# The second pair of batches boards one expert later, and an odd batch's last steps run without the next batch's first ones

## The chip, the cores and the metric

The kernel runs on one core of a Trainium2 chip. The metric is device time in microseconds of one execution, given as the median of several runs; less is better. One execution was also taken by the hardware profiler, and every row of a profile shown here comes from such an execution. TensorE is called PE in the rows (PEld for its weight loads), VectorE DVE, ScalarE ACT, GpSimd POOL, and SyncE, which issues nearly all DMAs, SP.

## What is computed

The input is x, 16 batches of 256 tokens by 256 channels, in float32. Four layers are added to it, one after the other:

```
x = x + L0(x)   # gates, 16 exponential moving averages over the tokens ("traces"), projections, layernorm
x = x + L1(x)   # masked softmax pooling over the 256 tokens of the batch
x = x + L2(x)   # 8 experts and a shared one, each silu(x Wg) * (x Wu) times Wd, width 1024, mixed by gates
x = x + L3(x)   # gelu(x W1 + b1) times W2, the last 64 columns with a matrix chosen by the batch
```

L0 and L1 need the tokens of one batch in order. L2 and L3 are matrix products with the same weights for all batches.

## The kernel before

Every float32 operand of a matrix product is split into a rounded part and a remainder, and each product is made of three matmuls (`mm3`, lines 101 to 103). The helper `rnd` (L88 on ACT) makes the rounded part, `low` (L95 on DVE or POOL) the remainder. Since all splits go through these helpers, rows are told apart by their tiles.

**The front end: steps.** For each batch b, L0 and L1 are two generators that yield after each step. `traces(b)` has 21 steps: the split of x and a scan (1), matmuls ph (2) and pm with a small store mdd (3), the gate matmuls pg with their activation and product gp (4), then sixteen steps with products bt (L359), scans tr (L363) and a running sum ta on POOL (L367), and a last split t (21). `pooled(b)` has 10 steps: matmuls pt (1), split s (2), matmuls po and statistics (3), x1 (L441, 4), transposes ptr (5), pa (6), psc and the exponentials (7), the normalisation (8), transposes ppt and the split q (9), and matmuls pp (L505 to L507), the sum acc (L509) and the split of acc, called x in the rows, its remainder on POOL (10). Except for batch 0, all PSUM results of these steps except the gate's gp share one tile with one buffer (tag `ps`).

**The back end: the plan.** L2 and L3 are a list of 640 items. An L2 item multiplies two 128-wide chunks of an expert's width by one batch, or one chunk by a pair of batches (512 columns either way). Its gate activation is L607, its product with the second half L608; its second matrix product comes two items later (`LAG`). An L3 item (activation L610) is an eighth of the last layer for a pair. Weight chunks arrive in a ring of ten buffers (`RING`), in the plan's order. On the first two uses of an expert's chunk it is loaded raw (raw_e, two buffers) and split; at the second it is stored split (keep_e), and from then on loaded split.

Experts go round in positions 0, 1, 2 ..., with position mod 9 the expert. A batch or a pair of batches boards at some position and rides nine positions, so that riders at the same position share the chunks. Batch 0 rides alone in positions 0 to 4, batches 0 and 1 together in 5 to 8, batch 1 alone in 9 to 13. Pair k (batches 2k and 2k+1) boards here:

```python
p0 = SECOND + NX * ((k - 1) // 2) + (0 if k % 2 else APART)
```

with NX = 9, APART = 5 and SECOND = 9. After a pair's last expert come its eight L3 items. Items are counted from 0 here, in the order of the plan; pair 1 boards at item 56, pair 2 at 128, pair 3 at 200, pair 5 at 360, pair 7 at 520.

**The order of the work.** The list `phases` says which steps are mixed: an entry with two generators takes steps of both in proportion (`feed`). `pace` gives how many steps follow each item, so that the steps due by `ready[b]` are done `SLACK` = 16 units of weight (an L2 item weighs 4, an L3 item 3) before the odd batch b boards. Where the next item is one of the first `HOLD` = 3 of an L3 group, no steps are given out. Each step's instructions are tied to come after the last item's product (`issue_after`); within that, a scheduler that works with its own estimate of times orders each engine's queue.

Of the kernel before, what the change touches and what calls it, by code (L numbers as in the profile page):

```python
# [23 lines left out]
FRONT = 4  # L24
SLACK = 16
L0_BUFS = {"bt": 3, "tr": 3, "mod": 2, "hA": 2, "hB": 2}
SECOND = 9
APART = 5
STORE = 2
LAG = 2  # L30
# [14 lines left out]
def fused_kernel(  # L45
# [662 lines left out]
    for k in range(1, NB // 2):  # L708
        p0 = SECOND + NX * ((k - 1) // 2) + (0 if k % 2 else APART)
        rides.append((p0, p0 + NX, (2 * k, 2 * k + 1)))  # L710
# [41 lines left out]
    phases, alone, ready = [[(traces, 0)]], {}, []  # L752
    count = FIRST
    for b in range(NB):
        more = b + 1 < NB
        phases.append([(pooled, b)] + [(traces, b + 1)] * more)
        count += STEPS["pooled"]
        if more and (b == 0 or b % 2):
            alone[len(phases) - 1] = FRONT
            phases.append([(traces, b + 1)])  # L760
            ready.append(count + FRONT)
            count += STEPS["traces"]
        else:
            count += STEPS["traces"] * more
            ready.append(count)
# [207 lines left out]
```

## Time and profile before

| | |
|---|---|
| median of 3 runs | 2857.16 us (2855.82 to 2858.89) |
| the profiled execution's own time | 2854.52 us |
| its span, first to last instruction | 2852.3 us |
| mean granted TensorE clock in it | 0.993 |
| PE busy / PEld busy | 2781.6 us (98%) / 2339.8 us (82%) |
| DVE / ACT / POOL busy | 1442.2 / 1239.2 / 1295.4 us |
| w_e loads from keep_e, of 768 KB each | 216 |
| raw_e loads, of 384 KB each | 144 |

Busy times are sums over the span, in which stages with different limits follow each other. A row of a timeline gives the start in us, the length in us, the engine, the line, the operation, the tiles written and read, and in brackets the idle time before it and what ended it. A row of waits gives who waited on whom, the total in us, how many times, and the longest.

### The profile page before, as it was taken

The page shows a single profiled execution, that of the slowest core. Times are in us where ns is not written, and L with a number is a line of the kernel's source. Part 1 is how long each engine was busy: PE and PEld are TensorE (multiplying, and loading weights), DVE is VectorE, ACT ScalarE, POOL GpSimd, SP SyncE. Part 2 cuts the span into 40 slices and gives each one's busy share as a digit, 9 for nine tenths or more (in the row PEclk, how much of TensorE's full clock was granted, in tenths as well). Part 3 has the DMA queues.
Part 4 walks back from the last instruction along what each step waited for, and adds up shares of the span by engine and source line. Part 5 has one row for each costly group of instructions (what it writes and reads, how often), then busy time and mean ns, then how long its engine had stood idle before and what let it go on. Part 6 is the DMA issues. An engine that isn't in the chain of part 4 may idle for free. (4 is left out here: it accounts for less than half of the span.)

```text
span 2852.3 us, 36958 instructions
## 1 busy us (share of the span) xinstructions
PE 2781.6 (98%) x13632; PEld 2339.8 (82%) x13632; DVE 1442.2 (51%) x2661; ACT 1239.2 (43%) x2054; POOL 1295.4 (45%) x984
## 2 busy tenths in 40 slices
PE   6889889999999999999999999999999999999999
PEld 4887778888888888888888888888888888888887
DVE  7978866665665454444544445444444542222222
ACT  5565544456444533435334443344433453233433
POOL 4755544544645453543534445344454443333333
PEclk8999999999999999999999999999999999999999
DMA  3444546547443532323433143332523242222552
GB/s 106 132 144 137 162 149 217 176 144 244 149 159 120 172 123 100 118 80 92 173 105 125 40 167 117 107 118 66 181 100 110 93 159 98 89 89 76 189 196 86
DMA packets 114694, 371.24 MB, mean 130 GB/s; under 512 B 12642, under 2 KB 30930, under 8 KB 114514
## 3 DMA queue, kind: packets, MB, share of 16 engines
q1 hardware_dynamic: 113650, 368.74, 39.0%
q8 instruction: 108, 1.77, 0.3%
q14 instruction: 72, 0.59, 0.1%
q10 hardware_dynamic: 864, 0.14, 0.0%
HBM read 304.62 MB, written 64.21 MB: 129 GB/s over the span
## 5 line engine op out<-in xcount | busy, mean ns | idle before, releaser
L95 POOL TENSOR_TENSOR hh<-h,hh 128x512 fp32r<-128x512 f32 x640 | 848.4, 1326 | 1327.1 <-ACT hh L88 1307.4
L608 DVE TENSOR_TENSOR h<-h,pu 128x512 f32<-128x512 f32 x576 | 393.9, 684 | 939.6 <-PE pu L103 818.1
L88 ACT ACTIVATE hh<-h 128x512 fp32r<-128x512 f32 x640 | 403.5, 631 | 932.6 <-DVE h L608 912.4
L101 PE MATMUL pg<-x,w_e 128*128 128x512 f32 (+1 forms) x1232 | 467.3, 379 | 12.7 <-ACT x L88 5.4
L607 ACT ACTIVATE h<-pg 128x512 f32<-128x512 f32 x576 | 342.9, 595 | 306.6 <-PE pg L103 228.5
L101 PE MATMUL pu<-x,w_e 128*128 128x512 f32 (+1 forms) x1232 | 465.4, 378 | 6.5 <-ACT h L607 3.7
L103 PE MATMUL pg<-x,w_e 128*128 128x512 f32 (+1 forms) x1232 | 465.7, 378 | 4.2 <-DVE w_e L95 3.4
L102 PE MATMUL y<-hh,w_e 128*128 128x512 f32 (+1 forms) x1232 | 464.4, 377 | 3.2 <-POOL hh L95 3.2
L102 PE MATMUL pg<-x,w_e 128*128 128x512 f32 (+1 forms) x1232 | 465.3, 378 | 0.0
L103 PE MATMUL pu<-x,w_e 128*128 128x512 f32 (+1 forms) x1232 | 463.8, 376 | 0.0
L102 PE MATMUL pu<-x,w_e 128*128 128x512 f32 (+1 forms) x1232 | 463.6, 376 | 0.0
L103 PE MATMUL y<-hh,w_e 128*128 128x512 f32 (+1 forms) x1232 | 463.5, 377 | 0.0
L101 PE MATMUL y<-hh,w_e 128*128 128x512 f32 (+1 forms) x1232 | 415.6, 377 | 1.0 <-DVE acc L655 0.8
L367 POOL TENSOR_TENSOR ta<-ta,tr 128x512 f32<-128x512 f32 x225 | 308.4, 1371 | 67.6 <-DVE tr L363 53.9
L363 DVE TENSOR_TENSOR_SCAN tr<-decay,bt 128x256 f32<-128x256 f32 x450 | 285.1, 672 | 0.0
L101 PEld LDWEIGHTS pg<-x,w_e 128*128 128x128 f32 x1232 | 232.5, 189 | 56.4 <-ACT w_e L88 6.4
L101 PEld LDWEIGHTS pu<-x,w_e 128*128 128x128 f32 x1232 | 232.1, 188 | 50.5 <-ACT h L607 5.8
L103 PEld LDWEIGHTS pg<-x,w_e 128*128 128x128 f32 x1232 | 232.7, 189 | 47.8 <-DVE w_e L95 5.2
L102 PEld LDWEIGHTS y<-hh,w_e 128*128 128x128 f32 x1232 | 233.0, 189 | 47.0 <-POOL hh L95 5.5
L101 PEld LDWEIGHTS y<-hh,w_e 128*128 128x128 f32 x1232 | 231.5, 189 | 44.8 <-ACT hh L88 1.3
L103 PEld LDWEIGHTS y<-hh,w_e 128*128 128x128 f32 x1232 | 233.0, 189 | 41.7
L103 PEld LDWEIGHTS pu<-x,w_e 128*128 128x128 f32 x1232 | 232.3, 189 | 41.9
(294 smaller groups left out, 3267.5 us busy)
## 6 DMA issues: line engine op xcount, KB each, us to landing
w_e<-keep_e SPq DMA_DIRECT2D x216, 768.0 KB, 4.4
raw_e<-in_wexp_dram SPq DMA_DIRECT2D x144, 384.0 KB, 4.5
keep_e<-w_e SPq DMA_DIRECT2D x72, 768.0 KB, 4.2
mod<-mdd SPq DMA_DIRECT2D x120, 256.0 KB, 3.5
w_f<-keep_f SPq DMA_DIRECT2D x56, 384.0 KB, 3.6
raw_c<-in_comb_dram SPq DMA_DIRECT2D x32, 260.0 KB, 2.8
xr<-in_xT_dram SPq DMA_DIRECT2D x16, 256.0 KB, 3.1
xt<-in_x_dram SPq DMA_DIRECT2D x16, 256.0 KB, 2.7
```

Source lines behind the costliest of these rows:

```text
L88: last_of["ca"] = A.activation(out_, in_, AF.Copy)
L95: i = (V if e == "v" else G).tensor_tensor(out_, in_, h.bitcast(F32), ALU.subtract)
L101: PE.matmul(o, wh, xh, start=start, stop=False, **kw)
L102: PE.matmul(o, wh, xl, start=False, stop=False, **kw)
L103: last_of["pe"] = PE.matmul(o, wl, xh, start=False, stop=stop, **kw)
L363: V.tensor_tensor_scan(tr[:, c], decay[:, d : d + 1].to_broadcast([P, S]), bt[:, c], 0.0, ALU.mult, ALU.add)
L367: G.tensor_tensor(tacc, tacc, tr, ALU.add)
L607: A.activation(h, ps_g, AF.Silu)
L608: last_of["h"] = V.tensor_tensor(h, h, ps_u, ALU.mult)
```

## The change

Two things are edited. `SECOND` goes from 9 to 10, so that pairs 1, 3, 5 and 7 as well as 2, 4 and 6 have a position that is one higher, and the plan has 46 positions in place of 45. And the entry of `phases` for `pooled(b)` with odd b no longer holds `traces(b + 1)`: those four steps (`FRONT`) come with the other 17 in the entry that follows. `ready` for odd b becomes four steps smaller. Batch 0 keeps its mixed entry, and so do the even batches.

```diff
-SECOND = 9
+SECOND = 10
...
     for b in range(NB):
         more = b + 1 < NB
-        phases.append([(pooled, b)] + [(traces, b + 1)] * more)
+        phases.append([(pooled, b)] + [(traces, b + 1)] * (more and (b == 0 or b % 2 == 0)))
         count += STEPS["pooled"]
         if more and (b == 0 or b % 2):
-            alone[len(phases) - 1] = FRONT
+            if b == 0:
+                alone[len(phases) - 1] = FRONT
             phases.append([(traces, b + 1)])
-            ready.append(count + FRONT)
+            ready.append(count + FRONT * (b == 0))
             count += STEPS["traces"]
         else:
             count += STEPS["traces"] * more
```

## The prediction

> **What bounds the kernel now.** I read the page first, then engine windows, then the waits and the timeline where TensorE stands still.
>
> ```profile
> span 2852.3 us, 36958 instructions
> ...
> PE 2781.6 (98%) x13632; PEld 2339.8 (82%) x13632; DVE 1442.2 (51%) x2661; ACT 1239.2 (43%) x2054; POOL 1295.4 (45%) x984
> ...
> PE   6889889999999999999999999999999999999999
> ```
>
> TensorE bounds the span, except in the first six or seven of 40 slices. The windows give the stages, and a stretch near the end in which no steps run:
>
> ```profile
> 76.00:198.00 122.00, 106.77 (x799) 100.17 (x798) 100.92 (x171) 72.04 (x113) 82.44 (x54) 0.97 0.48 144
> 198.00:360.00 162.00, 150.02 (x697) 119.90 (x696) 140.70 (x230) 86.96 (x141) 93.92 (x66) 0.99 0.47 149
> 360.00:380.00 20.00, 20.00 (x159) 19.48 (x158) 13.03 (x24) 12.30 (x21) 9.29 (x8) 1.00 0.60 197
> 380.00:404.00 24.00, 15.05 (x73) 12.61 (x73) 12.89 (x32) 6.31 (x12) 4.62 (x4) 0.79 0.20 64
> 404.00:718.00 314.00, 312.76 (x1765) 274.05 (x1763) 201.88 (x349) 163.08 (x269) 154.66 (x113) 1.00 0.56 190
> ...
> 2407.00:2668.00 261.00, 261.00 (x1153) 216.20 (x1152) 60.21 (x101) 81.47 (x134) 82.84 (x65) 1.00 0.26 85
> ```
>
> The columns are length, busy PE, PEld, DVE, ACT, POOL, granted clock, DMA share, GB/s. The worst window is 380 to 404: PE 15 of 24, PEld half, clock 0.79, and no other engine busy either: a chain of waits. To place it I count gate activations (L607; L610 in the last layer): the nth in time belongs to plan item n. Items 528 to 591 (2406.8 to 2667.9) run without steps, 64 in 261 us: an expert item costs **4.08 us**. Items 464 to 479 take 68.9 us with 12 steps: a hidden step costs TensorE (68.9 - 65.3)/12 = **0.3 us**. Item 55 has its gate at 375.3, item 56, the first of batches 2 and 3, at 404.1: **28.8 us in place of 4.1**.
>
> ```profile
> POOL x L95 <- ACT x L88: 19.4, 1, 19.4
> DVE gp L308 <- ACT gp L306: 6.5, 1, 6.5
> ACT gp L306 <- PE pg L103: 6.0, 1, 6.0
> ...
> PE pg L101 <- ACT x L88: 3.4, 1, 3.4
> ...
> PE pg L101 <- DVE q L95: 1.9, 1, 1.9
> ...
> PE pp L505 <- ACT gp L306: 1.0, 1, 1.0
> ```
>
> These are waits in that window (us, times, longest). POOL, ACT and PE all wait for x, the split of batch 3's sum. Why it is late, the timeline tells:
>
> ```profile
> 387.43 0.55 PE L101 MATMUL pg<-x,wh 128*128 128x256 f32 x1 [1.90 <-DVE q L95]
> ...
> 393.77 0.39 PE L505 MATMUL pp<-q,v 128*128 128x256 f32 x1 [1.02 <-ACT gp L306]
> ...
> 394.48 2.44 DVE L359 SCALAR_TENSOR_TENSOR bt<-gp,bl,mod 128x256 f32<-128x256 f32 x6
> ...
> 397.44 0.73 DVE L509 TENSOR_TENSOR acc<-x1T,pp 128x256 f32<-128x256 f32 x2
> ...
> 398.90 1.28 POOL L95 TENSOR_TENSOR x<-acc,x 128x512 fp32r<-128x512 f32 x1 [19.43 <-ACT x L88]
> ```
>
> The probabilities q are split at 387.3, but ahead of batch 3's last product pp stand the 24 gate matmuls pg of batch **4** (387.4 to 392.7), their activation, which frees the single PSUM tile, and on DVE batch 4's bt and scan work. pp starts at 393.8, the sum ends at 398.2. That foreign step costs batch 3's last step some **7 us**.
>
> **What the skill says.** "Perfetto Trace Analysis", section Matmuls, asks that independent groups rotate through PSUM banks; here traces and pooled share one tile (tag ps), and "PE pp <- ACT gp" above is that. Its section Sequencer Loop has an engine's instruction wait in its queue for semaphores; agreed: pp stands behind pg. "TensorE: Matmul & The Clock Gate", section What's actually happening, says an idle window of about 3.4 us halves the clock; agreed: clock 0.79, and pg matmuls of 256 columns stand 0.21 us apart at 388 against 0.12 for pp at 394. So a TensorE pause costs more than its length.
>
> **Part 1, boarding one expert later.** I worked plan, due times and steps through by hand from the listing. There are 640 items in both, total weight 2496. Batch 1's four items with expert 1 move ahead of pair 1, which boards at item 60 in place of 56; its eight shared items turn up after batch 0 and 1's last layer, as items 112 to 119. Pair 2 and all later ones board at the same item as before (128, 200, 288 ...). Cost: one expert position more (46 for 45), so eight more w_e loads of 768 KB, from the kept copy. The page has w_e loads at 4.4 us to landing, the DMA share in 2407 to 2668 is 0.26: taken as 0, at most 8 x (4.4 - 4.08) = 3 us if that cover went. A second cost lies in items 52 to 59, eight alone in a row, each two chunks of the ring, all split afresh. In the first stage, with the same diet, items 4 to 15 take 79.2 us, 6.6 each, and ACT waits for raw loads:
>
> ```profile
> ACT w_e L88 <- DMA raw_e<-in_wexp_dram: 51.0, 40, 3.5
> ```
>
> (waits of 76 to 360). The ring's ten chunks cover the first four; the other four I price at 6.6: 4 x (6.6 - 4.6) = 8 us; lower bound 0, if the ring is full, upper 16.
>
> **Part 2, no trace steps beside odd batches.** For b = 3, 5 ... 13 and 1, four steps of traces(b+1) move behind pooled(b): 32 PE matmuls (6 ph, 2 pm, 24 pg), 7 ACT activations, 6 DVE and one POOL operation, on SP the small mdd store, and the x loads of batch b+2 are asked ten steps later. Nothing vanishes: the same 488 steps. The moved work costs 0 where PE is full, the cover being the expert items; its loads (2.7 to 3.1 us landing) have a whole traces stage of 21 steps before use. In pair 1's wait it is worth the 7 us above. The pace falls as well: steps due by item 16 are 54 for 58, and until pair 1 boards (116 - 54)/(224 - 64) per unit of weight for (120 - 58)/(208 - 64), 1.55 per item for 1.72. DVE is busy 87% from 198 to 360, so fewer steps relieve it: item 49 has 105 steps behind it for 115. At TensorE's 0.3 us the ten are worth 3 us. At DVE's share, 140.7 less 32 items x 1.9 us (product 0.68 and chunk split 1.19, by their rows), over 55 steps, 1.45 us each, they are worth 14; but five of them fall in the first stage, which the chunk loads hold: 7. I take 6.
>
> **The sum for pair 1.** Item 49 comes at 345.9 - 6 = 340. Pooled 3 now has its steps in items 49 to 55. It began 29 us behind its item before (item 44 at 324, first pt at 352.7), dragged by pooled 2 in the DVE-bound stage; I take 15 (5 to 29). Its chain took 45.5 us (352.7 to 398.2), less 7: 38. From the sum to the gate took 5.9. So gate 60 comes at 340 + 15 + 38 + 6 = **399** (389 to 413). The TensorE side: eleven items from 49 at 4.6 are 51, and 8 for chunks: 399 too. So the wait should nearly close. Before, gate 60 came at 417.9: 19 earlier. Take off the seven steps still owed (120 for 127 at item 60), 2 us; pair 2's wait, items 120 to 127 in 43.1 us for 35, of which 5.7 come back right after, is worth 2 more, since pooled 5 stands free of traces(6). **19 us.** The profiled execution, 2854.5 with its span of 2852.3, becomes 2835.5; the median lies 2.7 above it: **2838**.
>
> **Rivals.** *A, forecast, 55%:* as summed, 2826 to 2847. *A', 6%:* half of it stays, 2848 to 2851.
> *B, the wait moves, 12%:* pooled 3 starts four items later in the plan; with the full 29 us lag and no 7 us saved, gate 60 comes at 340 + 29 + 45 + 6 = 420; two are owed, and 3.5 come back as they do today (gates 56 to 60 lie 13.8 apart for 17.3): no change, 2857. For it: lags of 35 to 50 us in pooled 2. Against: fewer steps, and pg gone from ahead of pp. That a planner orders each engine anyway, so that the trace steps were not the cause, ends here too.
> *C, slower, 17%:* the odd batches from 7 on. Pooled 7 had three steps before the last layer's hold; now all ten come in items 186 to 195, pair 3 boarding at 200. It has 963 to 1016, 5.2 us a step. Pooled 15, alone today, runs steps 4 to 10 in 2329.9 to 2362.1, 5.4 us each, and boards without a wait; but pooled 7 took 9.5 beside traces(8). Each us a step beyond 5.2 costs pairs 3, 5 and 7 some 10 + 8 + 9 us: from 5.9 the gain is gone; at 6.5, 35 - 19 = 16 us slower, 2873.
> *D, more, 10%:* the early lag vanishes and the chunks are in time: gate 60 at 389, with DVE's full relief of 14 at 381: 37 less the two owed: 2822.
>
> **The numbers.** A measurement of this kernel can tell 0.2%, 5.7 us, from no change. Faster: A, A' and D, 0.71; same: B, 0.12; slower: C, 0.17. The range 2818 to 2860 leaves out most of C and a tail of D.
>
> **What would show it.** Right: 224 w_e loads from keep_e for 216; gate 60 near 399, and no gap over 12 us from 55 to 60; no pg matmul between ppt and pp of batch 3; clock over 0.9 from 380 to 404; gate 128 some 19 us before 718.4. Wrong: gate 60 past 410, or ACT's waits for raw_e in front of items 56 to 59; and for C, gate 200 further from gate 128 than today's 302.6 us, with acc last.

## Result: 0.5% slower, where 0.7% faster was forecast

The changed kernel takes 2870.43 us in the median of six runs, against 2855.64 us for the kernel before in runs beside it: a ratio of 1.0049 (95% interval 1.0038 to 1.0059), some 14 us slower. One of the six runs took 7168.18 us; the ratio leaves it out, and the other five lie between 2868.65 and 2871.61. The forecast was 2838, with 2818 to 2860 as its range. The profiled execution of the change took 2871.61 us; its times below come from that one. First the page, lines as shown of the kernel before:

```profile
span 2869.7 us, 36970 instructions
...
PE 2786.8 (97%) x13632; PEld 2341.3 (82%) x13632; DVE 1441.6 (50%) x2661; ACT 1250.3 (44%) x2060; POOL 1297.0 (45%) x984
...
PE   6898989999999999999999999999999999999999
```

The same 13632 matmuls and the same DVE work take 17.4 us more. ACT is busy 11 us longer, 7.7 us of it in six more loads of its function tables (106 for 100, of 1.28 us each). PE is busy 5.2 us longer with the same matmuls; the other 12 us of the span are time in which it stood still. As forecast, there are 224 w_e loads from keep_e. The windows (columns as before: length, busy PE, PEld, DVE, ACT, POOL, granted clock, DMA share, GB/s):

```profile
76.00:198.00 122.00, 107.00 (x799) 99.04 (x799) 95.68 (x152) 73.31 (x113) 80.63 (x53) 1.00 0.45 138
198.00:360.00 162.00, 150.22 (x696) 120.50 (x695) 142.30 (x236) 84.20 (x133) 94.70 (x67) 0.98 0.48 149
...
398.00:425.00 27.00, 18.21 (x91) 15.84 (x90) 9.79 (x22) 12.71 (x25) 7.06 (x5) 0.75 0.43 144
```

DVE does 5.2 us less up to 198 us than before (95.7 for 100.9) and no less after that. And the pause in which no engine is full, which was to close, is still there, from 398 to 425, with the clock at 0.75. From 380 to 404 the clock is 1.00, as the forecast's signs asked, but only because the pause has moved. Who waits from 398 to 425:

```profile
POOL x L95 <- ACT x L88: 13.7, 1, 13.7
ACT x L88 <- DVE acc L509: 4.3, 1, 4.3
```

It is the same wait as before, for the split of batch 3's sum, and pair 1 is again what it holds up. Rows of the changed kernel's timeline (start, length, engine, line):

```profile
375.84 0.74 DVE L509 TENSOR_TENSOR acc<-x1T,pp 128x256 f32<-128x256 f32 x2
...
377.98 0.28 PE L101 MATMUL pt<-t,wh 128*128 128x256 f32 x1
...
398.67 0.58 ACT L607 ACTIVATE h<-pg 128x512 f32<-128x512 f32 x1
...
414.99 0.58 PE L505 MATMUL pp<-q,v 128*128 128x256 f32 x1 [1.81 <-DVE q L95]
...
417.95 0.75 DVE L509 TENSOR_TENSOR acc<-x1T,pp 128x256 f32<-128x256 f32 x2 [3.02 <-PE pp L507]
...
418.76 0.58 PE L101 MATMUL ph<-x,wh 128*128 128x256 f32 x1 [0.84 <-DVE acc L509]
...
424.94 0.60 ACT L607 ACTIVATE h<-pg 128x512 f32<-128x512 f32 x1
```

Batch 2's sum ends at 376.6 (before, at 348.4), batch 3's pooling begins at 378.0 (352.7) and takes 40.7 us to its sum at 418.7 (45.5). So the second edit does locally what it says: batch 4's first matmul ph now stands behind batch 3's sum, no foreign matmul stands ahead of pp. But the whole front end arrives some 25 us late. Gate 59 is at 398.7, gate 60 at 424.9: 26.3 us between two items, as there were 28.8 at item 55 before.

Where does the delay begin? At batch 2's start. The change first, then the kernel before (ph is the first matmul of batch 2's head, gp the end of its four first steps):

```profile
188.46 0.38 PE L101 MATMUL ph<-x,wh 128*128 128x256 f32 x1
...
209.38 0.69 DVE L308 SCALAR_TENSOR_TENSOR gp<-gp,xr 128x512 f32<-128x512 f32 x1
```

```profile
146.18 0.28 PE L101 MATMUL ph<-x,wh 128*128 128x256 f32 x1
...
180.29 0.69 DVE L308 SCALAR_TENSOR_TENSOR gp<-gp,xr 128x512 f32<-128x512 f32 x1
```

Batch 2's gated input is ready 29 us later. The edit of `phases` holds for b = 1 too, and b = 1 lies in the stage where TensorE is not the bound.

Against before, gate 60 is 7.0 us later, gate 128 5.1 (19 earlier was forecast), gate 144 12.8, gate 288 17.8, and from 528 on 17.4. So less than half of the loss is there at pair 1. From 430 to 2700 us PE stands still for 9.3 us, before for 2.3, and most of that is in three waits ahead of the last layer's second product z; before, no such wait is over 0.6 us:

```profile
630.21 0.47 PE L101 MATMUL z<-hh,w_f 128*128 128x512 f32 x1 [3.35 <-DVE acc L655]
...
1353.48 0.47 PE L101 MATMUL z<-hh,w_f 128*128 128x512 f32 x1 [2.06 <-DVE acc L655]
...
2035.61 0.47 PE L101 MATMUL z<-hh,w_f 128*128 128x512 f32 x1 [1.74 <-DVE acc L655]
```

### The profile page after: what moved, and what is told of

It is laid out like the page before. It is cut to its first block, busy times and chain, and to the rows that moved or that the text cites. A ratio compares the mean times of both kernels' runs of the same rounds, so it can differ in the third digit from the quotient of the medians.

```text
span 2869.7 us, 36970 instructions
## 1 busy us (share of the span) xinstructions
PE 2786.8 (97%) x13632; PEld 2341.3 (82%) x13632; DVE 1441.6 (50%) x2661; ACT 1250.3 (44%) x2060; POOL 1297.0 (45%) x984
```

## The experiments

The theories' numbers in the expectations: 1, that batch 3 just follows the pace set for it; 2, that the phases cost; 3, that eight lone items in a row hold the front end. Theory 2 later splits into 2a (the head behind batch 1's pooling, by its order), 2b (the later odd batches) and 2c (the due count of steps before pair 0 boards, `ready` of batch 1). Times stand against the kernel before, run beside them; its medians lay between 2854.28 and 2854.93.

**One edit at a time.** e1 has SECOND = 10 alone, e2 the phases alone (with their `ready`).

> SECOND = 10 alone, phases as before. Theory 1 (the pace follows the boarding: steps are given out so that batch 3 is done just before its item, and run some 43 us late, so a boarding four items later makes batch 3 four items later): acc of batch 3 ends at 412 to 422, gate 60 at 418 to 430, time +5 to +15 us against before. Theory 2 (the loss comes from the phases, odd batches without mixed trace steps): gate 60 at 395 to 408, time -5 to -20 us. Theory 3 (eight items alone in a row, with their 16 fresh chunk splits, hold DVE and ACT): gate 60 at 415 to 425 as well, time +5 to +10; run e3 tells it from theory 1.

Measured: 2846.92 us, ratio 0.9974 (0.9965 to 0.9982), 7 us faster. Batch 3's sum ends at 410.4, gate 60 is at 415.4.

> The new phases and ready with SECOND = 9. Theory 1: batch 3 boards at item 56 as before, its last step no longer behind batch 4's gate matmuls: acc of batch 3 ends at 388 to 396, gate 56 at 394 to 402, time 0 to -8 us. Theory 2: acc of batch 3 not before 405, gate 56 at 411 or later, time +5 to +15. Theory 3: as theory 1.

Measured: 2868.40 us, 1.0046 (1.0029 to 1.0063), 14 us slower. Batch 3's sum at 405.7, gate 56 at 411.6. Boarding later is a gain with the old phases and none with the new ones; the phases are the loss, with either boarding. That is theory 2, though e1's batch 3 is later than it said.

**The pace for pair 1.** e3 and e4 move batch 3's due time back to 208, e3 with the old phases, e4 with the new.

```diff
-    due = [(at[boards[b]] - SLACK, ready[b]) for b in range(1, NB, 2)]
+    due = [(at[boards[b]] - SLACK - 16 * (b == 3), ready[b]) for b in range(1, NB, 2)]
```

> SECOND = 10, phases as before, and the due time of batch 3 moved 16 units earlier, to 208, so that all steps up to item 52 are given out after the same items as before. Theory 1: acc of batch 3 ends at 396 to 404, as before (398.2), gate 60 at 402 to 410, time -8 to -16 us against before. Theory 3: batch 3's chain is held by the chunk splits of items 52 to 59: acc at 408 or later, gate 60 at 414 or later, time 0 to +8. Theory 2 says as theory 1 here.

Measured: 2844.90 us, 0.9967 (0.9955 to 0.9980), within noise of e1. Batch 3's sum ends at 409.6, not at 396 to 404; that is where theory 3 put it, but the time is not what theory 3 said.

> The whole change, with batch 3's due time back at 208. Theory 1: acc of batch 3 at 390 to 402, gate 60 at 396 to 408, time -5 to -18 us against before, 20 to 30 below the change. Theory 2: little better than the change, +8 to +14 against before. Theory 3: 0 to +8.

Measured: 2867.46 us, 1.0040 (1.0027 to 1.0052). Batch 3's sum at 418.0, as in the change. Giving the steps of batches 2 and 3 out earlier brings batch 3's sum forward by under 1 us in both: theory 1 falls.

**Which odd batches.** Four kernels with SECOND = 10 take the trace steps away beside some batches only: e6 beside 1, e7 beside 3, e8 beside 5 to 13, e9 beside 3 to 13. The edit of e7, against the kernel before, SECOND left out:

```diff
+        mix = more and not (b == 3)
-        phases.append([(pooled, b)] + [(traces, b + 1)] * more)
+        phases.append([(pooled, b)] + [(traces, b + 1)] * mix)
...
-            alone[len(phases) - 1] = FRONT
+            if mix:
+                alone[len(phases) - 1] = FRONT
...
-            ready.append(count + FRONT)
+            ready.append(count + FRONT * mix)
```

> SECOND = 10, and the trace steps are taken away beside batch 1 alone; beside batches 3 to 13 they stay. Theory 2a (the first four trace steps are a serial head of some 30 us that ran beside batch 1's pooling; put behind it they delay the whole front end, which has no slack until pair 1 boards): first sixteen-step product of batch 2 at 214 to 220 for 188, pooled 2 ends at 374 to 378 for 357 in e1, gate 60 at 425 to 440, time +8 to +20 us against e1, so 0 to +13 against before. Theory 2b (the loss is beside the later odd batches): within 3 us of e1, -4 to -10 against before.

Measured: 2863.29 us, 1.0030 (1.0020 to 1.0039), 16 us over e1. gp of batch 2 at 208.7, batch 2's sum at 376.8, gate 60 at 432.8, as theory 2a said.

> SECOND = 10, and the trace steps are taken away beside batch 3 alone. Theory 2a: pooled 3 starts as in e1 (358) and its chain falls from 52 us to 27 to 41, acc of batch 3 ends at 385 to 400; gate 60 at 396 to 408, time -14 to -24 us against before. Theory 2b: a loss against e1, so 0 to -5 against before.

Measured: 2839.06 us, 0.9946 (0.9930 to 0.9963), 16 us faster than before and 8 below e1. Batch 3's sum ends at 391.1, and the wait at pair 1 is gone. Pooled 3's first matmul, batch 3's sum, and gates 59 and 60 (of an execution that took 2835.03 us, the fastest of the four):

```profile
342.07 0.28 PE L101 MATMUL pt<-t,wh 128*128 128x256 f32 x1
...
390.41 0.74 DVE L509 TENSOR_TENSOR acc<-x1T,pp 128x256 f32<-128x256 f32 x2
...
392.80 0.58 ACT L607 ACTIVATE h<-pg 128x512 f32<-128x512 f32 x1
...
398.18 0.60 ACT L607 ACTIVATE h<-pg 128x512 f32<-128x512 f32 x1
```

The time and the gate are as theory 2a said, the way there is not: pooled 3 starts at 342.1, not 358, and takes 49.0 us, not 27 to 41 (e1: 357.9 and 52.5).

> SECOND = 10, and the trace steps are taken away beside batches 5 to 13, where TensorE has expert items to fill every wait. Theory 2a: nearly nothing there, within 3 us of e1, -4 to -10 against before; the gates of the change drift away by 6 us or so between items 144 and 448 as compared with before, and if that comes from these batches, it is +4 to +8 against e1, 0 to +1 against before. Theory 2b: +15 or more against e1.

Measured: 2854.66 us, 1.0000 (0.9991 to 1.0009), 7 us over e1: not nothing, so the drift of the change's gates does come from these batches.

> SECOND = 10, and the trace steps are taken away beside batches 3 to 13, not beside batch 1: the change without its effect on batch 1. Theory 2a: the forecast's own case, gate 60 at 396 to 408, time -8 to -22 us against before. Theory 2b: slower than e1 by 10 or more, so 0 to +8 against before.

Measured: 2847.45 us, 0.9974 (0.9963 to 0.9984): e7's gain less what e8 lost, and 1 us short of theory 2a's range. Gate 60 is at 402.0, near the 399 that the forecast summed.

So the edit of the phases is three things, each measured alone against e1: +16 us beside batch 1, -8 beside batch 3, +7 beside the later ones. They don't simply add: their sum is 16 us, and the change is 23.5 us over e1. One part of the difference shows in gate 60. Beside batch 3 the edit brings it forward by 17.2 us from e1 to e7, but the change, where batch 2's head is late, has it only 7.9 us before e6.

**Batch 1: order or due count?** e10 and e11 are e7 with three and eight trace steps beside batch 1 in place of four. e12 takes the steps away beside 1 and 3, but keeps 58 steps due before pair 0 boards.

> e7 with three trace steps beside batch 1 in place of four: the gate step of batch 2 goes behind batch 1's pooling. Theory 2a (serial head): that step and the way from it to the first product take some 16 us, so the first of batch 2's products comes at 200 to 206 for 186 in e7, gate 60 6 to 12 us later than 398, time +5 to +12 us against e7 (2839), so -3 to -11 against before. Theory 2c (it is the lower pace of the first 16 items, 54 steps for 58, that costs): one step of four, +4 or less against e7.

Measured: 2843.36 us, 0.9957 (0.9940 to 0.9973), 4 us over e7, though the runs of the two overlap. gp of batch 2 at 183.7 for 178.2; gate 60 at 402.3. That is nearer theory 2c.

> e7 with eight trace steps beside batch 1 in place of four, 62 steps due by the same item. Theory 2a: the head ran fully beside the pooling already; four more steps bring batch 2's products 5 to 10 us forward but load DVE before pair 0 boards: within 6 us of e7 either way, -10 to -22 against before. Theory 2c: a higher early pace helps again, 5 us or more below e7.

Measured: 2839.02 us, 0.9945 (0.9928 to 0.9961): as e7. gp of batch 2 at 154, 24 us earlier, and yet batch 3's sum ends at 395.1. That is theory 2a's case: what is gained at batch 2's head is lost again by then.

> No trace steps beside batches 1 and 3, SECOND = 10, and the steps due by the first boarding set to 58 as in the kernel before, so that the early pace is the old one. Theory 2a: batch 2's head still starts only when batch 1's pooling ends; the quicker pace may bring that end up to 5 us forward; first product at 205 to 216, time +6 to +16 against e7, so -9 to +1 against before. Theory 2c: back at e7 within 3 us, -13 to -18 against before.

Measured: 2843.18 us, 0.9957 (0.9941 to 0.9974), 4 us over e7. Batch 1's pooling, alone, begins at 126.9 and its sum ends at 168.2; gp of batch 2 at 184.2. Neither theory had this: the order costs 4 us (e7's runs lie between 2835.03 and 2840.29, e12's between 2840.65 and 2844.19), and the due count should cost more than that. Two kernels separate them.

```diff
# e14: the change, and
-            ready.append(count + FRONT * (b == 0))
+            ready.append(count + FRONT * (b == 0) + 4 * (b == 1))
# e15: SECOND = 10, the old phases, and
-            ready.append(count + FRONT)
+            ready.append(count + FRONT - 4 * (b == 1))
```

> The whole change, with one number put back: 58 steps due before pair 0 boards (item 16) in place of 54. Theory 2c (the due count costs most): first bt product of batch 2 at 184 to 188 for 210, gate 60 at 400 to 408, time 2846 to 2853, 17 to 24 us below the change and -1 to -9 against before. Theory 2a (the order costs most): within 8 us of the change, +6 to +14 against before.

Measured: 2852.21 us, 0.9987 (0.9981 to 0.9994), 18 us below the change, by one number, as theory 2c said. In the plan, worked through from the listing, the lower count puts batch 1's ten pooling steps behind items 10 to 15 in place of 9 to 13, and the head of batch 2 behind items 16 to 18 in place of 14 and 15. Its rows, batch 1's sum, batch 2's ph and gp:

```profile
169.23 0.75 DVE L509 TENSOR_TENSOR acc<-x1T,pp 128x256 f32<-128x256 f32 x2
...
172.12 0.28 PE L101 MATMUL ph<-x,wh 128*128 128x256 f32 x1
...
185.79 0.70 DVE L308 SCALAR_TENSOR_TENSOR gp<-gp,xr 128x512 f32<-128x512 f32 x1 [0.46 <-ACT gp L306]
```

In the change batch 1's sum is at 187.7:

```profile
187.67 0.74 DVE L509 TENSOR_TENSOR acc<-x1T,pp 128x256 f32<-128x256 f32 x2
```

> SECOND = 10 with the old order of steps, and 54 steps due before pair 0 boards in place of 58. Theory 2c: the mixed steps slip behind item 16, first bt product of batch 2 at 190 to 205, gate 60 at 420 to 432, time +8 to +16 us against e1 (2847), so 0 to +9 against before. Theory 2a: the head still runs beside the pooling, within 4 us of e1, -4 to -11 against before.

Measured: 2852.03 us, 0.9990 (0.9981 to 0.9998), 5 us over e1, between the two theories. gp of batch 2 at 188.2, gate 60 at 420.8. With the steps mixed, the lower count costs 5 us; with the head in a row behind the pooling it costs 18.

> e7 (trace steps taken away beside batch 3 alone, SECOND = 10) with 62 steps due before pair 0 boards in place of 58. Theory 2c, if it goes on: batch 2's products 6 to 10 us earlier, but e7's wait at pair 1 is closed on TensorE's side too (gates 52 to 60 in 43.4 us), so no more than 5 us: -15 to -21 against before. Else: within 3 us of e7, or slower as DVE fills before item 20.

Measured: 2840.67 us, 0.9952 (0.9936 to 0.9969), no better than e7: 58 is enough.

**The later batches.** e8's gates drift from e1's by 6.1 us. From 430 to 2700 us PE stands still for 8.3 us in e8 and for 1.8 in e1, which is all of the drift. Most of it lies before single matmuls: 2.8 us in two waits before pu from 600 to 700 us, and 2.0 and 1.8 before the first z of the last layer at 1334 and 2015 (e1: under 0.6 before any z). The longer wait before pu is on ACT (e8's timeline, with PE's row last), where the exponentials of batch 5's pooling come in between two gates:

```profile
677.04 1.28 ACT L477 ACT_TABLE_LOAD   x1
678.34 0.51 ACT L477 ACTIVATE sc<-sc,mx 128x256 f32<-128x256 f32 x1
...
678.96 1.28 ACT L607 ACT_TABLE_LOAD   x1
680.25 0.60 ACT L607 ACTIVATE h<-pg 128x512 f32<-128x512 f32 x1
...
680.90 0.50 PE L101 MATMUL pu<-x,w_e 128*128 128x512 f32 x1 [2.02 <-ACT h L607]
```

Two table loads and an exponential take 3.2 us before the gate runs, and pu waits for the gate. The waits before z are on DVE (e9's timeline, which shows them as well, with 1.7 and 1.8 us on PE):

```profile
1329.60 0.15 DVE L548 COPY bias<-raw_c 128x1 f32<-128x1 f32 x1 [2.56 <-DMA raw_c<-in_comb_dram]
1329.67 1.65 DVE L655 SCALAR_TENSOR_TENSOR acc<-y,coef,acc 128x256 f32<-128x256 f32 x4
```

A copy of one column waits 2.6 us for its load, and the sums behind it free the y tiles that z needs. The Trainium skill's "Perfetto Trace Analysis", section Sequencer Loop, says that an engine's instruction waits for its semaphores; here the ones behind it wait too, those 2.6 us. e13 is e9 with that copy on ACT.

```diff
-                V.tensor_copy(bias3[:, b : b + 1], raw[:, 512:513])
+                A.activation(bias3[:, b : b + 1], raw[:, 512:513], AF.Copy)
```

> e9 (trace steps taken away beside batches 3 to 13, SECOND = 10) with the small copy of the last layer's bias (L548) on ACT in place of DVE, so that DVE's queue no longer stands at that copy's load ahead of the sum that frees the y tiles. If the stalls of 2.0 and 1.7 us on PE before the first z matmul of pairs 2 and 4 come from that copy, they fall under 0.7 each and the time is 2 to 4 us below e9 (2847.5). If they come from the pooling's own DVE work, they stay.

Measured: 2841.33 us, 0.9955 (0.9938 to 0.9971), 6 us below e9. PE's waits for acc at 1329 and 2010, 1.7 and 1.8 us in e9, are gone. They are not the whole 6 us: between the two profiled executions 2.0 us are there at gate 60 already, before the first of these copies runs (547 us in e13), and where those come from is open. A third wait before z, at pair 0's last layer, stays at 5.5 us (the wait on PE, in e13):

```profile
PE z L101 <- DVE acc L655: 5.5, 1, 5.5
```

There DVE is busy with trace products and scans of the next batch ahead of the sums, not with the copy. e9's own row is 5.4, and e7 has no such stall. The change has all three waits before z, as shown above. So what e8 and e9 lose is seen in rows; whether these stalls come from the scheduler's other order of the queues, or from the place of the steps as such, was not tried.

## Why the prediction was wrong

**Right: where the kernel was bound. Right in the number, in part by luck: the sum for pair 1.** The pause at pair 1 and the foreign gate matmuls ahead of pp are as described. e7, the change at batch 3 without the rest of the phases' edit, has gate 60 at 398.2 for 399 and takes 2839 us for the 2838 forecast. But two terms of that sum were off and cancelled: pooled 3 starts level with item 49 (342.1 and 342.5), for a lag of 15, and takes 49.0 us for 38. The foreign step was priced at 7 us; pooled 3 is shorter by 3.5 us from e1 to e7 and by 7.2 from e6 to the change. Most of e7's gain at gate 60 is that pooled 3 starts 16 us earlier than in e1, since batch 2's pooling took 102 us for 117. That is ahead of the place that was edited, and why it is shorter is not shown. The eight added loads cost nothing that shows: e1 has them and is 7 us faster.

**Wrong: "The moved work costs 0 where PE is full".** It lists b = 1 among the places and then prices all of them by a cover that b = 1 has not: up to 198 us PE is busy 107 of 122 us at best, and the front end is what pair 1 will wait for. Put behind batch 1's pooling, the head costs 4 us by its order alone (e12) and 16 with the due count that falls with it (e6). Beside batches 5 to 13 PE is full (in e1 busy for 2268.2 of the 2270 us from 430), and still the move costs 7 us (e8).

**Wrong: the relief from the pace, 6 us off item 49.** The prediction read "54 steps due by item 16 for 58" as fewer steps in the way, a gain; e14 against the change shows that it costs 18 us. Item 49 did come at 342.1 for 345.9, 4 us early, but e7, with 58 due, has it at 342.5, so it is not the lower count that brings it. And those four steps are the head of batch 2: on the plan they moved from items 9 to 15 to items 16 to 18. What follows varies much less than when it starts. From the start of gp of batch 2 to the end of batch 3's sum:

| kernel | gp of batch 2 | sum of batch 3 | between | gate 60 |
|---|---|---|---|---|
| before | 180.3 | 398.2 | 218 | 417.9 |
| e1 | 181.8 | 410.4 | 229 | 415.4 |
| e3 | 182.2 | 409.6 | 227 | 414.6 |
| e15 | 188.2 | 414.5 | 226 | 420.8 |
| e6 | 208.7 | 426.3 | 218 | 432.8 |
| e7 | 178.2 | 391.1 | 213 | 398.2 |
| e12 | 184.2 | 395.3 | 211 | 404.0 |
| e14 | 185.8 | 396.7 | 211 | 405.3 |
| e4 | 207.8 | 418.0 | 210 | 424.1 |
| the change | 209.4 | 418.7 | 209 | 424.9 |

Where the steps beside batch 3 are taken away and SECOND is 10, it is 209 to 213 us (e9, e10, e13 and e16 too); where they stay, it is 226 to 229 (e8 too), save in e6 with 218. The pace set for batch 3 moves it by 1 us (e3 against e1, e4 against the change). So the lag that I took to fall from 29 us to 15 was 36 (pooled 3 at 378.0, item 49 at 342.1): a lag against the plan is no stretch that a slower plan makes good. Where a whole stretch of the front end runs at its own speed, giving out its first steps later only lets it start later. e11 marks the limit: started 24 us earlier still, it takes 241, and nothing is won.

**Half wrong: the chunk price.** Before, with boarding at item 56, the stretch is 218 us, in e1 229; without the steps beside batch 3, e2 has 197 and the change 209. So boarding later costs the front end 11 to 12 us, where I had priced the lone items at 8 on TensorE's side only. That it is the fresh chunk splits was not tried by itself.

**Wrong in size: rival C.** The measured time came near its 2873, by another way. Half of its sign came: from gate 128 to gate 200 there are 308.9 us for 302.6, 6 more, and gate 200 stands 9.8 us behind gate 199, for 4.7. Its mechanism, pairs 3, 5 and 7 waiting, did not show: PE is busy for all of those 9.8 us, and batch 7's pooling took 48 us from pt to its sum, for 81 before, as hoped. The later batches cost 7 to 9 us all the same (e8 against e1, e14 against e12), in the ACT and DVE queues, which the prediction did not price at all.

The account, from e7 to the change: 2839.1; the order beside batch 1, +4.1 (e12); the order beside 5 to 13, +9.0 (e14); four steps no longer due before item 16, +18.2. That is 2870.4; the terms add up because each kernel is the one before it with one thing more, and another order would share them out otherwise (alone, the lower count costs 5 us in e15). The forecast, 2838, priced the two orders at nothing and counted the lower count within a gain of 6 us.

**A version that beats both.** e7: SECOND = 10, and the trace steps taken away beside batch 3 alone, 2839.06 us. e11 is level with it.

## What to carry to other kernels

When a deadline is eased, ask first which chain has no slack before it. A count of "work due by here" that drops with a change of order is itself an edit, and in a stage that the side work bounds, it can cost more than the order (18 us and 4 us here). Where one edit holds for every turn of a loop, price the turns by stage: here the same line was worth +16, -8 and +7 us in three of them. And where a sum comes out, look at its terms in the trace: in e7 two of them were wrong by 11 and 15 us and cancelled.

## What the runs showed of the hardware that I had not expected

A one-column copy on DVE, 0.15 us of work, held TensorE up by 1.7 to 2.0 us twice in e8 and in e9, since it waited for its load with the sums behind it; in e13, with the copy on ACT, both waits are gone. A switch of ACT from the gate's function to the exponential and back cost two table loads of 1.28 us each in e8, and with the exponential itself 3.2 us before the next gate. And the granted clock fell to 0.75 in the pause from 398 to 425 us, where pp's matmuls of 256 columns stood 0.21 us apart, as in the pause of the kernel before.
